# A grouped-scan convolution block on one core: one pair of units reordered where the pipeline fills, and two GpSimd outputs moved ahead of additions in the tail

## The chip, the cores and the metric

The kernel runs on one NeuronCore of one Trainium2 chip. The metric is device time in microseconds of one launch; the time before is the median of three runs. Engines are called PE (TensorE), DVE (VectorE), ACT (ScalarE), POOL (GpSimd) and SP (SyncE, which issues the DMAs here).

## The reference, cut to what matters

`x` is (4, 128, 96, 96) in float32. After a group norm, each of the four images is read as a sequence in four orders (rows, rows backward, columns, columns backward). On each sequence of 9216 positions a gated state-space block runs, and the four results are put back in place, joined by `fuse_w` and added to `x`:

```python
t = _grouped1x1(x, in_proj_w, in_proj_b, G)            # 128 -> 512, 4 groups
u, gate = t[:, :HID], t[:, HID:]
u = silu(u)
u = depthwise_conv(u, dw_w)                            # 5 taps along the sequence
s = _conv1x1(u, ssm_in_w)                              # 256 -> 32
a = DMIN + (DMAX - DMIN) * sigmoid(_conv1x1(u, ssm_delta_w, ssm_delta_b))
bb = tanh(_conv1x1(u, ssm_b_w, ssm_b_b))
cc = tanh(_conv1x1(u, ssm_c_w, ssm_c_b))
prefix = cumsum(log(a))
hst = exp(prefix) * cumsum(bb * s * exp(-prefix))      # h[n] = a[n] h[n-1] + bb[n] s[n]
u = u + _conv1x1(cc * hst + ssm_d[None, :, None] * s, ssm_out_w)
u = _grouped1x1(u * sigmoid(gate), mix_w, mix_b, G)
return _conv1x1(u, out_proj_w, out_proj_b)
...
x = x + fuse(concatenate(four results))
```

## The kernel before

**Units and pairs.** There are 8 phases: 4 images, each once as "V" and once as "H". A phase has 6 steps of 16 lines, and a step has 4 pairs. A pair is two units that run together, one forward (`s` = 0) and one backward (`s` = 1), each of N = 384 positions: every fourth position of a step, so that the phase of a position in the sequence is a separate array. In all there are 384 units and 192 pairs; `pair(t)` is called for t = 0 to 191, then `tail()`. The unit of pair t is i = 2t. Work on a unit is spread over pairs: `pair(t)` computes the front of pair t + 4, the convolution and projections of pair t, the scan results of pair t − 5, and the gates, state products and gating of pair t − LAG, with LAG = 6. The unit of that last one is called `bi`. So pair 6 is the first with `bi` = 0, the first in which gates and state products appear.

**Order.** All engines run in program order (`manual_schedule`), so the order of the calls is the order of each engine's queue, and an instruction that waits holds up all behind it. Waits are put in by the framework from the tiles and regions that instructions touch.

**What a pair does.** `front` makes four in_proj products per pair (L134, tiles of 32x32) into four PSUM banks, and ACT applies SiLU to each (L470). The depthwise convolution is done in two halves: channels of block 0 by PE with band matrices (`conv`, then `conv_less`), evicted by ACT to `u` (L616 or L618); channels of block 1 by DVE in taps (`taps`: the first tap by ACT at L635, four more by DVE at L637, in PSUM banks 0 and 1). `proj` makes s, a, bb and cc (L134 psum<-u,main), read by ACT at L674, L675 and L680; POOL multiplies them into the scan's inputs (L682, L683). DVE scans (L709), two halves per step. `outputs` forms cc * h and adds d * s: a multiplication (L715), an addition (L716) and a copy (L718), as a rule on POOL. `out_of` is the state product (L504, contraction of 32 rows), `gate` the product for the gate (L491, 32 rows), `sigmoids` the tanh of the gates (L521), `gating` the DVE work u = (gate + 1) * (u + state product) (L583 and L584). From pair 8 on `under` copies u into the PSUM bank ahead of the state product, and L583 is not needed. `accumulate` is the last product (L134 psum<-u,w_fin: mix, out_proj and fuse are one matrix), evicted by ACT as `ys` (L742, L744) and added to `acc` by POOL (L761), or added from PSUM by DVE (also L761) where `last` is set. `scale_s` is L692.

**PSUM.** There are 8 banks, given out by hand. Banks 0 to 3 hold the state products of the pair being gated (`SSM`), banks 0 and 1 also the taps. `FRONT` = (7, 6, 2, 3) are the banks of the front, `PROJ` = (4, 5) those of the convolution and projections, `GATE[True]` = (6, 4, 5, 7) those of the gates where a front runs in the same pair. So a bank passes several times in one pair from PE to ACT or DVE and back.

**Pair 6.** Here `bi` = 0 and a front is computed (step 2, group 2, called front 10 below; pair 7 computes front 11). The order of calls is `front(10, FRONT)`, taps and `conv`, `conv_less` with two copies, `outputs(2)`, `gates_and_out(0, True)`, `gating` of both units, `first_tap(14)`, `proj(12)`, `scale_s(10)`.

**Tail.** It finishes the pairs 186 to 191. `gate_units(n)` is the gating of pair n with `under` of pair n + 1; `product(n, 0, 4)` the last product of its forward unit into bank 4, added by POOL; `product(n, 1, 5)` that of the backward unit into bank 5, added by DVE when `add()` is called, which also issues the stores that are due; `z_copy` (L916) copies the scan result to the other half of the partitions for the state products. Two additions of pair 185 are held (`adds`). The outputs of pair 189 (`outputs(378, None, nc.vector)`) are on DVE, those of units 376, 380 and 382 on POOL:

```python
        ssm_out(first + 1)
        for held_add in adds:
            held_add()
        gate_units(first + 1)
        outputs(2 * first + 6, None, nc.vector)
        outputs(2 * first + 8, None)
        product(first, 0, 4)
        product(first, 1, 5)
        z_copy(first + 2)
        product(first + 1, 0, 4)
        outputs(2 * first + 10, None)
        add()
```

Here `first` = 186, so 2 * first + 6 is unit 378, + 8 unit 380 and + 10 unit 382.

Of the kernel before, what the change touches and what calls it, by code (L numbers as in the profile page):

```python
# [56 lines left out]
R = 4  # L57
LN = 16
NS = HH // LN
N = LN * WW // R  # L60
# [7 lines left out]
def conv_preact_kernel(  # L68
# [9 lines left out]
    nc = tc.nc  # L78
# [41 lines left out]
    psum = ps.tile([P, 8, 512], F32, name="psum")  # L120
    SSM, TAPS, PROJ = 0, 0, (4, 5)
# [379 lines left out]
    def out_of(bi, s, j):  # L501
        z = tbs[bi]
        r = slice(64 * j + 32 * s, 64 * j + 32 * s + 32)
        nc.tensor.matmul(bank(ssm(bi, s) + j)[:, :N], w_so[r, bass.ts(j, P)], z[r, :],  # L504
                         start=bi not in seeded, stop=True, skip_group_check=True)
# [8 lines left out]
    def sigmoids(bi, to):  # L514
        bn = stats[units[bi]["b"]][1]
        n = bi // 2
        gv = gates[n % 2]
        for s in range(2):

            for j in (0, 1) if s == 0 or to[0] == GATE[True][0] else (1, 0):  # L520
                nc.scalar.activation(  # L521
                    gv[:, s, j, :],
                    bank(to[2 * s + j])[:, :N],
                    AF.Tanh,
                    bias=bn[:, 2 + j : 3 + j],
                    scale=0.5,
                )
            load_gate(bi + s + UB)
        if n % NP < NP // 2 - 2:
            nc.sync.dma_start(kept[n // NP % 2][n % NP], gv)  # L530
# [19 lines left out]

    def gates_and_out(bi, with_front):

        to = GATE[with_front]
        gate(bi, 0, 0, to[0])
        gate(bi, 0, 1, to[1])
        if with_front:
            gate(bi, 1, 0, to[2])
            out_of(bi, 1, 0)
            out_of(bi, 0, 0)
            out_of(bi, 0, 1)  # L560
            out_of(bi, 1, 1)
            gate(bi, 1, 1, to[3])
        else:

            out_of(bi, 1, 0)
            gate(bi, 1, 0, to[2])
            out_of(bi, 1, 1)
            out_of(bi, 0, 1)
            out_of(bi, 0, 0)
            gate(bi, 1, 1, to[3])  # L570
        sigmoids(bi, to)

    def gating(bi, s):

        v = units[bi + s]["v"] = us[bi][:, s]
        m = mirror(bi // 2)
        if m is None:
            g = gates[bi // 2 % 2][:, s]
        else:
            g = old_gates.get(bi // 2, gates[m % 2])[:, 1 - s, :, ::-1]  # L580
        pz = psum[:, ssm(bi, s) : ssm(bi, s) + 2, :N]
        if bi not in seeded:
            nc.vector.tensor_add(pz, pz, v)  # L583
        nc.vector.scalar_tensor_tensor(v, g, 1.0, pz, ALU.add, ALU.mult)  # L584

# [20 lines left out]
    def conv_less(i, banks):  # L606
        step, p = units[i]["step"], units[i]["p"]
        sil, k, b0 = blocks(step), less_of(p), min(banks)
        for g in range(4):
            for s in range(2):  # L610
                r = less_rows(s, p)
                mm(bank(b0 + s), g, less[r, p, g, :], columns(step, sil[s][r, g, :], k),
                   False, True)
        if banks == PROJ:
            for s in range(2):
                nc.scalar.copy(us[i][:, s, 0, :], bank(b0 + s)[:, :N])  # L616
        else:
            nc.scalar.copy(us[i][:, :, 0, :], psum[:, b0 : b0 + 2, :N])  # L618
# [94 lines left out]
    def outputs(i, copy=nc.gpsimd.tensor_copy, engine=nc.gpsimd, r=slice(0, N)):  # L713
        ta, tb, p = scans[units[i]["step"]], tbs[i], units[i]["p"]
        engine.tensor_mul(ta[0:64, p, r], tb[64:P, r], ta[64:P, p, r])  # L715
        engine.tensor_add(tb[0:64, r], ta[0:64, p, r], tb[0:64, r])  # L716
        if copy:
            copy(tb[64:P, :], tb[0:64, :])  # L718
# [65 lines left out]
    def pair(t):  # L784
        i, k, bi = 2 * t, t % R, 2 * (t - LAG)
        back = bi >= 0
        old = back and mirror(bi // 2) is not None

        late = bi > 2 and (bi - 2) % (NU // B) == 0
        with_front = fresh((t + R) // R)  # L790
        final = (nc.vector, True) if t == NU // 2 - 1 else ()
        seed = old or back and not with_front

        ahead = old or back and not with_front
        banks, w = plan(with_front or not back)
        if not back:
            banks = head_banks(t)
        if back:
            front(t + R, FRONT)
        for n in soon:  # L800
            load_kept(n)
        soon.clear()
        if seed and not with_front:
            under(bi, 1)
        if t < NU // 2 - 2:
            send()

        if len(reload) == 4 and (k == 1 or late):
            for b, r in reload:
                nc.sync.dma_start(accf[:, r], xr[b, :, r])  # L810
            reload.clear()
        if t:
            new_u(i)
            taps(i, range(1, K))
            conv(i, banks)
        if t and not ahead:
            conv_less(i, banks)
        if not back and t:
            first_tap(i + 2)
            front(t + R, FRONT if banks == PROJ else (5, 4, 2, 3))  # L820
        recurrence(t)
        un = units[i]
        stats_chunks(t)

        ending = old and t % (2 * NP) > NP + NP // 2

        def stats_piece(at_end=False):
            if later and k > 1 and at_end == ending and t % (2 * NP) not in (27, 39):
                next(later[0], None)

        if not ahead:
            free[0] = w[1]
            stats_piece()
        if seed and with_front:
            for s in (1, 0):
                under(bi, s)
        for add in held:
            add()
        held.clear()
        if waiting:  # L840
            add = accumulate(waiting.pop(0), w[0], *final)
            if late:
                held.append(add)
            else:
                add()

        between = ahead and not old
        if between:
            conv_less(i, banks)
        if seed and not with_front:  # L850
            under(bi, 0)
        if ahead:
            accumulate(waiting.pop(0), w[1], *final)()
            free[0] = w[0]
            stats_piece()
            if not between:
                conv_less(i, banks)
        if old:
            scale_s(i - 2)
            for s in range(2):  # L860
                for j in range(2):
                    out_of(bi, s, j)
                load_gate(bi + s + UB)
        elif back:
            gates_and_out(bi, with_front)
        if back:
            for s in range(2):
                gating(bi, s)
        if un["order"] == "V" and un["b"] + 1 < B and un["st"] == NS - 1 and k == R - 1:
            later[:] = [stats_finish(un["b"] + 1)]  # L870
        if t + 2 < NU // 2:
            load_chunks(t + 2)
        if back:

            if k == 2 and t + 1 < NU // 2:
                soon.append(bi // 2 + 2)
            else:
                load_kept(bi // 2 + 2)
            if waiting:
                add = accumulate(waiting.pop(0), w[1])  # L880
                if late:
                    held.append(add)
                else:
                    add()
            first_tap(i + 2)
        if t == NU // 2 - 1:
            for s in range(2):
                under(bi + 2, s)
        if t == NU // 2 - 1:
            outputs(i - 8, None)  # L890
        if ending:
            free[0] = FRONT[0]
            stats_piece(True)
        proj(i, PROJ if back else banks, between)
        if not old and t > 0:
            scale_s(i - 2)
        if back:
            waiting.extend(units[bi : bi + 2])
        if t >= NU // 2 - 4:
            load_last(t)  # L900

        if bi > 0 and bi % (NU // B) == 0:
            send()

    def tail():
# [4 lines left out]
        def ssm_out(n):  # L910
            for s in range(2):
                for j in range(2):
                    out_of(2 * n, s, j)
# [24 lines left out]
        for part in range(2):  # L938
            scan(NU // UB - 1, part)
            outputs(2 * first + 4, None, r=bass.ts(part, N // 2))  # L940
        ssm_out(first + 1)
        for held_add in adds:
            held_add()
        gate_units(first + 1)
        outputs(2 * first + 6, None, nc.vector)
        outputs(2 * first + 8, None)
        product(first, 0, 4)
        product(first, 1, 5)
        z_copy(first + 2)
        product(first + 1, 0, 4)  # L950
        outputs(2 * first + 10, None)
        add()
        ssm_out(first + 2)
        for n in range(first + 2, end - 1):
# [226 lines left out]
```

## Time and profile before

| | |
|---|---|
| Median of 3 runs | 1815.12 us (1814.3 to 1817.42) |
| Profiled execution | 1815.66 us, its span 1813.9 us |
| Mean granted PE clock | 0.999 |
| Instructions | 56969, of them 24090 matmuls and as many weight loads |
| DMA | 321.17 MB, mean 177 GB/s |

The span runs from the first instruction to the last; the profiled execution's own time is longer by what lies around it. "Busy" is the time in which an engine executes, and PE's ends are modelled, so PE's busy time does not say that it runs at its peak. A timeline line gives start and length in us, engine, source line, operation, written and read tiles, shapes and count, and in brackets the idle time before it with what ended that. A line of waits gives who waited for whom, then total us, count and longest. A line of windows gives the stretch and its length, then busy us and instruction count of PE, PEld (weight loads), DVE, ACT and POOL, then the granted PE clock, the DMA share and GB/s.

### The profile page before, as it was taken

Reading aid. Unit: us, or ns where it says so; the run is one execution under the profiler, and the core shown is the slowest. Engines: PE = TensorE matmul, PEld = TensorE weight load, DVE = VectorE, ACT = ScalarE, POOL = GpSimd, SP = SyncE. Lnnn points to the kernel's source line nnn. Section 1 sums busy time; section 2 is a strip of 40 time slices with the busy share of each in tenths; the row PEclk is TensorE's granted clock in tenths of the full one; section 3 lists DMA queues with packets and bytes.
Section 4 is the critical chain, followed back from the end, with each engine's and each line's share of the span. In section 5 each row is a group of like instructions: output and inputs, shape, how many; then the busy total and the mean of one; then the engine's idle time right before and its main releaser. Section 6 shows DMA issues by size and latency. Waiting matters only on the chain.

```text
span 1813.9 us, 56969 instructions
## 1 busy us (share of the span) xinstructions
PE 1788.7 (99%) x24090; PEld 643.7 (35%) x24090; DVE 1448.5 (80%) x1462; ACT 1562.6 (86%) x2750; POOL 1431.1 (79%) x1477
## 2 busy tenths in 40 slices
PE   7999999999999999999999999999999999999998
PEld 3333333333333333333333333333333333333333
DVE  6888878787888887877778888787877788777886
ACT  4888888988888888898888888889888888888975
POOL 3587888788778888787877888878877788887786
PEclk9999999999999999999999999999999999999999
DMA  8555463444975466344696456443476634635434
GB/s 247 178 188 180 148 195 107 162 144 155 314 239 186 158 186 183 113 139 139 221 300 226 144 176 207 127 164 118 159 237 220 232 142 138 197 102 180 149 123 158
DMA packets 148047, 321.17 MB, mean 177 GB/s; under 512 B 14160, under 2 KB 115920, under 8 KB 147792
## 3 DMA queue, kind: packets, MB, share of 16 engines
q1 hardware_dynamic: 147648, 317.48, 54.1%
q8 instruction: 190, 3.11, 0.7%
q14 instruction: 65, 0.53, 0.1%
q10 hardware_dynamic: 144, 0.04, 0.0%
HBM read 185.21 MB, written 132.25 MB: 175 GB/s over the span
## 4 chain that ended last, share of the span: by engine, by line
PE 94%; DVE 2%; DMA 2%; ACT 1%; issue 0%; POOL 0%; SPq 0%; DVEq 0%; ACTq 0%; POOLq 0%
PE psum L134 81%; PE psum L504 8%; PE psum L491 5%; DVE psum L637 1%; DMA x_in<-in_xs 1%; DMA xs<-in_xr 1%; DVE u L584 0%; DMA acc<-in_xr 0%; DVE u L637 0%; ACT psum L635 0%; ACT psum L512 0%; ACT u L618 0%; ACT sil L470 0%; DVE t L715 0%; DVE t L709 0%
## 5 line engine op out<-in xcount | busy, mean ns | idle before, releaser
L637 DVE SCALAR_TENSOR_TENSOR psum<-sil,small,psum 128x768 f32<-128x768 f32 x576 | 589.0, 1022 | 28.3 <-ACT psum L635 3.4
L584 DVE SCALAR_TENSOR_TENSOR u<-gate,psum 128x768 f32<-128x768 f32 x376 | 349.6, 952 | 273.9 <-ACT u L616 122.4
L134 PE MATMUL psum<-u,w_fin 128*32 128x384 f32 (+1 forms) x6192 | 552.7, 486 | 3.5 <-DVE acc L761 2.1
L134 PE MATMUL psum<-u,main 128*32 128x384 f32 x6144 | 534.7, 489 | 1.2 <-DVE u L637 1.2
L761 POOL TENSOR_TENSOR acc<-ys,acc 128x384 f32<-128x384 f32 x375 | 411.7, 1119 | 27.9 <-ACT ys L744 8.4
L715 POOL TENSOR_TENSOR t<-t,t 64x384 f32<-64x384 f32 (+1 forms) x192 | 237.3, 1236 | 157.0 <-DVE t L709 73.3
L134 PEld LDWEIGHTS psum<-u,w_fin 128*32 128x32 f32 x6192 | 189.7, 110 | 322.6 <-issue 215.2
L134 PEld LDWEIGHTS psum<-u,main 128*32 128x32 f32 x6144 | 181.9, 109 | 324.5 <-issue 196.8
L512 ACT COPY psum<-u 128x768 f32<-128x768 f32 x352 | 276.8, 799 | 19.2 <-DVE u L637 11.3
L134 PE MATMUL psum<-sil,band 128*32 128x384 f32 x3072 | 285.1, 488 | 0.0
L682 POOL TENSOR_SCALAR t<-tm 64x384 f32<-64x384 f32 x191 | 177.0, 926 | 118.1 <-ACT tm L674 98.9
L716 POOL TENSOR_TENSOR t<-t,t 64x384 f32<-64x384 f32 (+1 forms) x192 | 248.8, 1296 | 15.1
L504 PE MATMUL psum<-t,main 32*128 32x384 f32 x1536 | 239.2, 513 | 1.3 <-ACT psum L512 0.6
L635 ACT ACTIVATE psum<-sil,small 128x768 f32<-128x768 f32 x191 | 173.2, 907 | 58.0 <-DVE u L584 49.7
L521 ACT ACTIVATE gate<-psum,bnorm 128x384 f32<-128x384 f32 x384 | 191.7, 581 | 27.0 <-PE psum L491 25.5
L683 POOL TENSOR_TENSOR t<-t,tm 64x384 f32<-64x384 f32 x192 | 195.1, 1016 | 15.3
L637 DVE SCALAR_TENSOR_TENSOR u<-sil,small,psum 128x768 f32<-128x768 f32 x192 | 194.9, 1015 | 7.8
L470 ACT ACTIVATE sil<-psum,bnorm 128x385 f32<-128x385 f32 x384 | 191.8, 584 | 3.9 <-PE psum L134 1.8
L134 PE MATMUL psum<-sil,less 64*32 64x384 f32 x3072 | 168.2, 495 | 0.0
L491 PE MATMUL psum<-x_in,wn 32*128 32x384 f32 x768 | 157.5, 527 | 0.4 <-ACT u L616 0.4
L134 PEld LDWEIGHTS psum<-sil,band 128*32 128x32 f32 x3072 | 90.6, 109 | 169.2 <-issue 95.0
L718 POOL COPY t<-t 64x384 f32<-64x384 f32 x187 | 136.5, 730 | 11.9
(102 smaller groups left out, 1477.2 us busy)
## 6 DMA issues: line engine op xcount, KB each, us to landing
sil<-sil SPq DMA_DIRECT2D x128, 770.0 KB, 6.9
kept<-gate SPq DMA_DIRECT2D x80, 768.0 KB, 3.7
gate<-kept SPq DMA_DIRECT2D x76, 768.0 KB, 4.8
x_in<-in_xs SPq DMA_DIRECT2D x192, 96.2 KB, 2.5
out<-acc SPq DMA_DIRECT2D x48, 384.0 KB, 8.5
acc<-in_xr SPq DMA_DIRECT2D x39, 384.0 KB, 6.4
xs<-in_xr SPq DMA_DIRECT2D x72, 192.0 KB, 5.8
x_in<-in_xs SPq DMA_DIRECT2D x46, 192.5 KB, 3.5
```

What stands on the lines that cost most here:

```text
L134: nc.tensor.matmul(o[r, : rhs.shape[-1]], lhsT, rhs, start=start, stop=stop, skip_group_check=True)
L470: nc.scalar.activation(sils[step][:, s, j, g, :], bank(bk)[:, : N + 1], AF.Silu, bias=bn[:, 1:2] if j else bn[:, 4 + g : 5 + g],)
L491: nc.tensor.matmul(bank(to)[:, :N], stats[un["b"]][0][r, s, :], x_in[s][r, q, off : off + N], start=True, stop=True)
L504: nc.tensor.matmul(bank(ssm(bi, s) + j)[:, :N], w_so[r, bass.ts(j, P)], z[r, :], start=bi not in seeded, stop=True, skip_group_check=True)
L512: nc.scalar.copy(psum[:, ssm(bi, s) : ssm(bi, s) + 2, :N], us[bi][:, s])
L521: nc.scalar.activation(gv[:, s, j, :], bank(to[2 * s + j])[:, :N], AF.Tanh, bias=bn[:, 2 + j : 3 + j], scale=0.5,)
L584: nc.vector.scalar_tensor_tensor(v, g, 1.0, pz, ALU.add, ALU.mult)
L637: nc.vector.scalar_tensor_tensor(us[i][:, :, 1, :] if k == K - 1 else part, src, w_tap[:, k : k + 1], part, ALU.mult, ALU.add,)
L683: nc.gpsimd.tensor_mul(ta[0:64, p, :], tb[0:64, :], tm[0:64, :])
L715: engine.tensor_mul(ta[0:64, p, r], tb[64:P, r], ta[64:P, p, r])
L716: engine.tensor_add(tb[0:64, r], ta[0:64, p, r], tb[0:64, r])
L761: adder.tensor_add(part, y, part)
```

## The change

In pair 6 (`bi` = 0) the front is computed in three pieces. Its in_proj goes into banks (2, 3, 7, 6) instead of (7, 6, 2, 3). The first two SiLUs, those of banks 2 and 3, stay ahead of the convolution; the other two come after `conv_less` and its copies. The four state products go ahead of the four gates, the gates use banks (4, 5, 7, 6), and DVE adds u to both units' state products before the first gating product. The change in `sigmoids` keeps the tanhs' order for this new set of banks at (0, 1). All other pairs are as before.

In the tail, `outputs` of unit 380 goes ahead of the two held additions, and `outputs` of unit 382 ahead of the products of pair 186 and 187, and so ahead of their additions on POOL. Nothing is added or taken out.

```diff
-            for j in (0, 1) if s == 0 or to[0] == GATE[True][0] else (1, 0):
+            for j in (1, 0) if s and to == GATE[False] else (0, 1):
...
     def gates_and_out(bi, with_front):
-        to = GATE[with_front]
+        to = GATE[with_front] if bi else (4, 5, 7, 6)
+        if bi == 0:
+            for s in range(2):
+                for j in range(2):
+                    out_of(bi, s, j)
+            for s in range(2):
+                for j in range(2):
+                    gate(bi, s, j, to[2 * s + j])
+            sigmoids(bi, to)
+            return
...
         pz = psum[:, ssm(bi, s) : ssm(bi, s) + 2, :N]
-        if bi not in seeded:
+        if bi == 0 and s == 0:
+            for e in range(2):
+                pe = psum[:, SSM + 2 * e : SSM + 2 * e + 2, :N]
+                nc.vector.tensor_add(pe, pe, us[bi][:, e])
+        elif bi and bi not in seeded:
             nc.vector.tensor_add(pz, pz, v)
...
-        if back:
+        if bi == 0:
+            turned = front_parts(t + R, (2, 3, 7, 6), half=True)
+            next(turned)
+            next(turned)
+        elif back:
             front(t + R, FRONT)
...
             conv_less(i, banks)
+        if bi == 0:
+            for _ in turned:
+                pass
...
         ssm_out(first + 1)
+        outputs(2 * first + 8, None)
         for held_add in adds:
             held_add()
         gate_units(first + 1)
         outputs(2 * first + 6, None, nc.vector)
-        outputs(2 * first + 8, None)
+        outputs(2 * first + 10, None)
         product(first, 0, 4)
         product(first, 1, 5)
         z_copy(first + 2)
         product(first + 1, 0, 4)
-        outputs(2 * first + 10, None)
         add()
```

## The prediction

> **What bounds the kernel now.** First the page: busy time, then the chain that ended last.
>
> ```profile
> PE 1788.7 (99%) x24090; PEld 643.7 (35%) x24090; DVE 1448.5 (80%) x1462; ACT 1562.6 (86%) x2750; POOL 1431.1 (79%) x1477
> ...
> PE 94%; DVE 2%; DMA 2%; ACT 1%; issue 0%; POOL 0%; SPq 0%; DVEq 0%; ACTq 0%; POOLq 0%
> ```
>
> The reader is to see that TensorE sets the time nearly everywhere: a change elsewhere pays only where PE stands still. So the next view is PE's waits, from 60 us to the end.
>
> ```profile
> PE psum L134 <- DVE acc L761: 2.1, 1, 2.1
> PE psum L134 <- ACT ys L742: 1.2, 1, 1.2
> PE psum L504 <- ACT psum L512: 0.6, 1, 0.6
> PE psum L134 <- DVE u L584: 0.6, 1, 0.6
> PE psum L491 <- ACT u L616: 0.4, 1, 0.4
> ```
>
> In 1750 us there are six waits, and three of them (2.1, 0.6, 0.4) lie where the change works: two in pair 6, one in the tail. PE's ends are modelled about 0.5 us late, so I count from start to start. PE's timeline in pair 6:
>
> ```profile
> 72.88 0.96 PE L491 MATMUL psum<-x_in,wn 32*128 32x384 f32 x2 [0.40 <-ACT u L616]
> ...
> 74.75 2.79 PE L134 MATMUL psum<-u,main 128*32 128x384 f32 x32
> 77.47 0.88 PE L134 MATMUL psum<-x_in,wn 32*32 32x385 f32 x16
> 78.92 0.88 PE L134 MATMUL psum<-x_in,wn 32*32 32x385 f32 x16 [0.57 <-DVE u L584]
> 79.73 0.53 PE L134 MATMUL psum<-sil,band 128*32 128x384 f32 x4
> ```
>
> The gates and state products start at 71.57 and projection at 74.75, 3.18 us later; in pair 7 the same stretch takes 1.58 (83.39 to 84.97). Then in_proj of front 11 is cut in two: banks 2 and 3 are held until VectorE's last product of the gating (L584) ends at 78.86. From conv (69.28) to conv (79.73) pair 6 takes 10.45 us. ScalarE in that stretch:
>
> ```profile
> 70.46 2.00 ACT L470 ACTIVATE sil<-psum,bnorm 128x385 f32<-128x385 f32 x4
> 72.33 0.88 ACT L616 COPY u<-psum 128x384 f32<-128x384 f32 x2
> 73.06 2.50 ACT L521 ACTIVATE gate<-psum,bnorm 128x384 f32<-128x384 f32 x4
> ```
>
> Four SiLUs stand ahead of the copies of u that free banks 4 and 5, and the gates wait for those banks. In the tail, VectorE and GpSimd:
>
> ```profile
> 1787.54 2.81 DVE L715 TENSOR_TENSOR t<-t,t 64x384 f32<-64x384 f32 x1
> 1787.65 1.95 POOL L761 TENSOR_TENSOR acc<-ys,acc 128x384 f32<-128x384 f32 x2
> ...
> 1789.67 1.73 POOL L715 TENSOR_TENSOR t<-t,t 64x384 f32<-64x384 f32 x1
> ...
> 1790.38 1.63 DVE L716 TENSOR_TENSOR t<-t,t 64x384 f32<-64x384 f32 x1
> ...
> 1791.94 0.54 DVE L761 TENSOR_TENSOR acc<-psum,acc 128x384 f32<-128x384 f32 x1
> ...
> 1792.53 0.87 PE L134 MATMUL psum<-u,w_fin 128*32 128x384 f32 x4 [2.14 <-DVE acc L761]
> ```
>
> VectorE's outputs of unit 378 (L715, L716) take 4.47 us, the addition that frees bank 5 is queued behind them, and PE waits for it. The clock by stretch adds a second price:
>
> ```profile
> 1788.88:1792.29 3.41, 1.51 (x18) 0.31 (x8) 3.38 (x3) 1.28 (x2) 3.25 (x3) 1.00 0.01 4
> 1792.29:1795.71 3.42, 3.18 (x20) 0.99 (x24) 2.23 (x4) 1.31 (x2) 3.34 (x4) 0.50 0.02 5
> ```
>
> After the wait PE runs at half clock (0.50) for 3.4 us. Its two products take 4.26 us there (1792.53 to the next L504 at 1796.79), the same work at full clock 2.72.
>
> **What the Trainium skill says.** "SBUF — State Buffer", Who interferes with whom: a VectorE instruction with two inputs in SBUF and a GpSimd one that reads SBUF exclude each other for the whole instruction. The trace agrees: VectorE's L715 ends 0.75 us after the second GpSimd addition, its L716 0.61 us after GpSimd's L715. "TensorE: Matmul & The Clock Gate", What's actually happening: the clock halves after an idle window of about 3.4 us on a free-running grid. The trace shows the same length (3.41 us at 0.50), but 2.1 us of idleness was enough here; 1.3 us (before 1788.04) was not. "TensorEngine Tiling (Array Packing)", Key Properties: matmuls on different row strips run side by side, and a change of tiling mode drains. Agrees: four state products on four strips take 0.86 us in the tail (1796.79 to 1797.65).
>
> **Pair 6, step by step.** Nothing is added or removed but the order and the banks.
> 1. ScalarE: SiLUs (0,0) and (0,1) at 70.46 to 71.52 as before. Conv_less starts at 70.71; in pair 7 the first copy of u follows its start by 0.97, so here at 71.68, not 72.33. The copies end at 72.16 and 72.54. SiLUs (1,0), (1,1) come after them, each 0.47 after the last: ends 73.01 and 73.48.
> 2. PE: the four state products need banks 0 to 3: last tap 71.35, SiLU (0,1) 71.52. They run at 71.57 to 72.33. The gates then wait for their banks one after another: 4 (72.2), 5 (72.6), 7 (73.05), 6 (73.52). From the last gate to projection it was 0.74 (74.01 to 74.75), so 73.52 + 0.74 = 74.3 against 74.75: only 0.45 saved, since the last SiLUs are now what is late.
> 3. VectorE: both additions run while ScalarE is at the gates: state products finish at 72.5, additions end 73.5 and 74.35. Tanhs end at 73.94, 74.41, 74.88, 75.35. So L584 ends at 75.4 and 76.35 instead of 76.93 and 78.86. Taps of pair 7, queued behind, end near 80.5, not 82.96.
> 4. In_proj of front 11 at 74.3 + 2.72 = 77.0: its banks 7, 6, 2, 3 are free at 76.35, so it runs whole, 0.97 as in pair 6. Conv at 77.98 against 79.73: **1.75 us saved**. Bank 5 for its second half: projection ends about 77.1, and the two ScalarE reads end at 78.2, before 78.6.
> The following SiLUs end at 80.8, so pair 7's copies of u end at 81.55, just before its gates at 81.6: nothing lost. Bounds: 0 if one of these banks is late, 2.6 if nothing waits (10.45 less 7.8 of PE work); I take 1.75. SP's queue keeps its order; the save of an older SiLU and the gate loads stay where they were, and their rows are needed four pairs on. From pair 8 on PE has no wait until the tail, so the gain is kept.
>
> **The tail.** Two mul and add pairs of GpSimd (2.4 us each) go ahead of the additions; no instruction is new.
> 1. VectorE's L715 is issued at 1787.54, while GpSimd's last half output runs to 1787.68. GpSimd's next was an addition, starting 0.03 before the end of the last, and so was the one after: VectorE got nothing until 1789.60. Now the next is a multiplication (L715), and ahead of each of those GpSimd leaves 0.08 us (1789.60 to 1789.67, 1786.15 to 1786.23): VectorE gets in, at about 1787.65.
> 2. VectorE's L715 ends near 1788.4 (0.61 to 0.75 after release), GpSimd's L715 near 1789.45 (1.06 later, as before), VectorE's L716 enters the gap there and ends near 1790.05 (0.61), not 1792.01. The addition ends at 1790.55 and PE starts at 1790.6 instead of 1792.53: **1.93 us**. PE itself is ready at 1790.33 (L504 at 1789.47 plus 0.86), so a faster VectorE would bring only 0.27 more. VectorE alone run without GpSimd is not in the trace; the bounds 0.5 and 0.95 give 1.7 to 2.1.
> 3. PE is then idle for 0.3 us, not 2.1, so the half clock should go: 4.26 − 2.72 = **1.54 us**. Bounds 0 and 1.7 (half of 3.41).
> 4. What is delayed: the held additions end near 1793.0 (were 1789.6), the next two at 1797.4 (were 1794.9). Their readers: the buffers of ys are wanted again at about 1793.5 and 1797, and four stores on SP start at 1797.4, taking some 4.5 us, before the last stores at about 1804. Both covered. Additions on VectorE touch other rows or columns of acc. Afterwards each unit takes 3.58 us as now.
>
> **Sum.** The profiled execution took 1815.66 (span 1813.9 and 1.8 around it). 1815.66 − 1.75 − 1.93 − 1.54 = 1810.44. It lies 0.5 above the median 1815.12, inside the runs shown (1814.3 to 1817.42); whether the half clock falls in every run isn't known, and a median run without it gains less from a lower start. I take **1810.4**.
>
> **Rivals.**
> B, only pair 6 pays: the tail's wait moves from the addition to another resource, or the reorder does nothing for VectorE. Against: the gap before each L715. 1815.66 − 1.75 = 1813.9.
> C, only the tail pays: a SiLU after the copies makes the last gate late, up to 0.9 us on PE. For: step 2 leaves ScalarE the limit. 1815.66 − 3.47 = 1812.2.
> D, slower: VectorE loses the gap. If its L715 comes after GpSimd's at 1787.76 (0.22 later than now), it ends at 1789.6, its L716 stands behind GpSimd's L716, both held additions (no gap between) and, if that gap is lost too, the multiplication of 382: 1794.35. PE at 1794.9 is 2.4 late, with the half clock up to 0.15 dearer; if pair 6 then brings nothing, 1818.2, with its gain 1816.5. Against: both engines are timed from the end of the same scan (1785.65).
>
> **Chances.** A 0.72 (1809.3 to 1811.8), B 0.10, C 0.09, D 0.09. 0.2% is 3.6 us, about what a measurement of this kernel can tell from no change: faster lies below 1811.5, which holds nearly nine tenths of A and a little of C, 0.64; slower, above 1818.75, a D that loses more than reckoned, 0.04; the rest 0.32. The range 1808.9 to 1813.3 leaves out D, most of B and a thin lower end of A, 0.2 in all.
>
> **What would show it.** Right: conv to conv in pair 6 near 8.7 us, no wait for L584; VectorE's L715 and L716 together 2.5 us, PE's wait for L761 under 0.4, no 0.50 clock before 1800. Wrong: projection of pair 6 after 74.75, a VectorE L716 over 2 us, or a new wait for ys or bank 6.

## The result, and the profile after

The changed kernel takes 1811.53 us (median of 13 runs, 1809.72 to 1817.25), the kernel before 1815.39 in as many runs (1814.03 to 1817.58): ratio 0.9978, 95% interval 0.9971 to 0.9986. That is 3.9 us less, by the interval 2.5 to 5.3; the forecast was 1810.4, 5.2 below the execution it was reckoned from. The profiled execution took 1814.41 us, with a span of 1812.7.

The page after, busy time:

```profile
PE 1788.9 (99%) x24090; PEld 645.3 (36%) x24090; DVE 1446.5 (80%) x1462; ACT 1567.0 (86%) x2750; POOL 1432.0 (79%) x1477
```

Counts of instructions and busy times are nearly those of before, as they should be for a change of order. What has changed is where PE stands still. PE's waits from 60 us to the end (who waited for whom, total us, times, longest):

```profile
PE psum L134 <- ACT ys L755: 1.2, 1, 1.2
PE psum L504 <- ACT psum L512: 0.6, 1, 0.6
PE psum L134 <- DVE acc L774: 0.3, 1, 0.3
PE psum L134 <- ACT t L693: 0.2, 1, 0.2
```

Lines have moved down: L742 is L755 now, L761 is L774, L583 and L584 are L596 and L597, L616 is L629, L715 and L716 are L728 and L729. Of the three waits that the prediction aimed at, the 2.1 us of the tail are 0.3 and those of pair 6 (0.6 and 0.4) are gone. PE's timeline in pair 6, and below it one line each of ScalarE's and VectorE's:

```profile
72.99 1.50 PE L134 MATMUL psum<-sil,band 128*32 128x384 f32 x16
...
75.23 0.96 PE L504 MATMUL psum<-t,main 32*128 32x384 f32 x8
75.98 2.18 PE L491 MATMUL psum<-x_in,wn 32*128 32x384 f32 x8
78.09 2.79 PE L134 MATMUL psum<-u,main 128*32 128x384 f32 x32
80.81 0.94 PE L134 MATMUL psum<-x_in,wn 32*32 32x385 f32 x32
81.69 1.50 PE L134 MATMUL psum<-sil,band 128*32 128x384 f32 x16
```

```profile
75.39 0.86 ACT L629 COPY u<-psum 128x384 f32<-128x384 f32 x2 [0.16 <-PE psum L134]
...
78.18 1.90 DVE L597 SCALAR_TENSOR_TENSOR u<-gate,psum 128x768 f32<-128x768 f32 x2
```

The state products run first and wait for nothing, in_proj stands in one block of 32, and from conv (72.99) to conv (81.69) it is 8.70 us where it was 10.45. VectorE's last gating product (L597) is done at 80.08, before in_proj asks for its bank. Pair 7 then takes 9.20 us (next conv at 90.89), 0.07 more than before. Both pairs together gain 19.58 − 17.90 = 1.68 us.

In the tail, VectorE, then GpSimd, then PE (start, length, engine, line, operation, tiles):

```profile
1789.79 0.89 DVE L728 TENSOR_TENSOR t<-t,t 64x384 f32<-64x384 f32 x1
1790.71 1.68 DVE L729 TENSOR_TENSOR t<-t,t 64x384 f32<-64x384 f32 x1
1792.32 0.53 DVE L774 TENSOR_TENSOR acc<-psum,acc 128x384 f32<-128x384 f32 x1
...
1790.02 1.74 POOL L728 TENSOR_TENSOR t<-t,t 64x384 f32<-64x384 f32 x1
...
1792.90 2.79 PE L134 MATMUL psum<-u,w_fin 128*32 128x384 f32 x32 [0.26 <-DVE acc L774]
```

VectorE's multiplication takes 0.89 us instead of 2.81: it gets in ahead of GpSimd's multiplication, where before it stood behind two GpSimd additions (e4 below tests this). Since all kernels differ a little at their start, tail times below are counted from the end of the last scan. PE's product, which waited for the addition, starts at 5.00 (before: 6.88), a gain of 1.88. It runs at full clock: 2.72 us to the next L504, where the profiled execution of before had 4.26. The tail ends 24.79 after the scan, before 28.22.

One thing in this profile was not in the forecast, whose sign "no 0.50 clock before 1800" holds in the tail alone. The windows around 26 us (stretch, length, busy us of PE, PEld, DVE, ACT, POOL, then the granted clock):

```profile
22.47:25.88 3.41, 2.97 (x90) 1.54 (x97) 0.85 (x5) 2.35 (x6) 0.00 (x0) 1.00 0.64 160
25.88:32.71 6.83, 6.83 (x70) 4.63 (x55) 0.99 (x6) 4.79 (x10) 0.81 (x1) 0.50 0.28 76
```

This execution spends 6.83 us at half clock while the pipeline fills, long before the changed code, and the conv of pair 5 starts at 66.14 instead of 62.45. Half clock for 6.83 us can cost up to 3.4 of these 3.69 us, an estimate from the window above. So its span is only 1.2 us shorter although pair 6 and the tail together gain 1.68 + 3.43. Counted from the conv of pair 5 to the end of the span, the kernel takes 1746.56 us, before 1751.42: 4.86 less.

### The profile page after: what moved, and what is told of

Its sections match the earlier page's. It is cut to its first block, busy times and chain, and to the rows that moved or that the text cites. A ratio compares the mean times of both kernels' runs of the same rounds, so it can differ in the third digit from the quotient of the medians.

```text
span 1812.7 us, 56970 instructions
## 1 busy us (share of the span) xinstructions
PE 1788.9 (99%) x24090; PEld 645.3 (36%) x24090; DVE 1446.5 (80%) x1462; ACT 1567.0 (86%) x2750; POOL 1432.0 (79%) x1477
## 4 chain that ended last, share of the span: by engine, by line
PE 95%; DMA 2%; DVE 2%; ACT 1%; issue 0%; SPq 0%; DVEq 0%
PE psum L134 82%; PE psum L504 8%; PE psum L491 5%; DVE psum L650 1%; DMA x_in<-in_xs 1%; DMA xs<-in_xr 1%; DMA acc<-in_xr 0%; DVE u L597 0%; DVE u L650 0%; ACT psum L512 0%; PE psum L1035 0%; ACT u L631 0%; SPq L296 0%; ACT ys L757 0%; DVE bn L387 0%
## 5 line engine op out<-in xcount | busy, mean ns | idle before, releaser
L597 DVE SCALAR_TENSOR_TENSOR u<-gate,psum 128x768 f32<-128x768 f32 x376 | 350.0, 953 | 273.4 <-ACT u L629 119.0
L774 POOL TENSOR_TENSOR acc<-ys,acc 128x384 f32<-128x384 f32 x375 | 411.6, 1119 | 24.0 <-ACT ys L757 7.9
L728 POOL TENSOR_TENSOR t<-t,t 64x384 f32<-64x384 f32 (+1 forms) x192 | 237.7, 1238 | 156.9 <-DVE t L722 73.2
L729 POOL TENSOR_TENSOR t<-t,t 64x384 f32<-64x384 f32 (+1 forms) x192 | 249.1, 1297 | 15.0
L504 PE MATMUL psum<-t,main 32*128 32x384 f32 x1536 | 238.6, 513 | 1.3 <-ACT psum L512 0.6
```

The costliest lines, as they stand in the source:

```text
L774: adder.tensor_add(part, y, part)
```

## The experiments

**Each part alone.** e1 keeps pair 6 as changed and the tail of before; e2 keeps pair 6 of before and the changed tail. e1, against the changed kernel:

```diff
         ssm_out(first + 1)
-        outputs(2 * first + 8, None)
...
-        outputs(2 * first + 10, None)
+        outputs(2 * first + 8, None)
...
         product(first + 1, 0, 4)
+        outputs(2 * first + 10, None)
```

> Only pair 6 is changed, the tail is that of before. Theory (two separate parts, each worth its own PE stall): conv to conv of pair 6 is 8.70 us as in the changed kernel, PE waits about 2.1 us for the DVE addition in the tail, and the time is 1.75 us below before (ratio 0.9990). Rival B': the gain of pair 6 is given back later by a transfer or by the tail, then the ratio is 1.000 though the stretch of pair 6 is short. Its trace is also one more look at whether PE falls to half clock after the 2.1 us wait.

> Only the tail is changed, pair 6 is that of before. Theory: pair 6 takes 10.45 us, PE's wait for the DVE addition is 0.3 us, no half clock there; the time is 1.9 us below before in executions of before without the half clock and 3.4 us in those with it, so between 0.9981 and 0.9990 as a ratio. Rival: the tail pays only together with pair 6 (a shifted phase of engines), then the wait of 2.1 us is back.

e1: 1812.6 us median, ratio 0.999 (0.9982 to 0.9998). Conv to conv is 8.70 and pair 7 9.19, and of this gain nothing is lost on the way: from the conv of pair 5 to that of pair 191, e1 takes 1.68 us less than the profiled execution of before. The tail is that of before (VectorE's multiplication 2.76 us, PE at 6.83, half clock after it). e2: 1811.72, ratio 0.9986 (0.9978 to 0.9994). Pair 6 takes 10.46; PE's product starts at 5.00 and the tail ends at 24.79, both exactly as in the changed kernel. The kernel before had 1814.3 beside both. So both parts pay and neither depends on the other: rivals B and C, with one part each, fall.

**Is it the half clock?** e3 leaves the kernel before as it is and fills PE's wait in the tail with two matmuls on weights whose sums nobody reads:

```diff
         ssm_out(first + 2)
+        for _ in range(2):
+            nc.tensor.matmul(bank(4), w_main[:, 0:P], w_main[:, 0:512], start=True, stop=True)
```

> The kernel before, with two matmuls of 128x512 on weights added into bank 4 after the state products of pair 188, in the time in which PE stood still for 2.1 us; their result is overwritten by the next product. Theory (the half clock comes of the idle time): PE still waits for the DVE addition and starts at the same distance from the scan, but runs at full clock, 2.72 us from that start to the next state products and not 4.26; the time is 0 to 1.5 us below before, by how often before falls to half clock. Rival (the half clock comes of something else, such as the stores or DVE and POOL at work): still 0.50 for 3.4 us, and the time 0 to 0.3 us above before.

The window that holds the wait, and PE's product after it, both of e3:

```profile
1795.35:1798.76 3.41, 3.20 (x24) 1.12 (x28) 3.41 (x4) 0.93 (x2) 3.33 (x3) 1.00 0.02 5
```

```profile
1797.42 2.79 PE L134 MATMUL psum<-u,w_fin 128*32 128x384 f32 x32 [0.21 <-DVE acc L761]
```

The product starts at 6.87 as in the kernel before, yet runs at full clock, and the tail ends at 26.67, 1.55 us sooner. Without the two matmuls PE would have stood still for 2.07 us of that one window (1795.35 to 1797.42), about as long as in b2 below, whose clock fell. So the half clock there comes of PE's idleness. But the timed gain is nothing that can be seen: 1813.53, ratio 0.9999 (0.999 to 1.0007). A saving of 1.5 us in every run would be 0.9992; the interval just holds that too, so the times alone don't settle it. They raise the question whether every run of the kernel before has a half clock there to lose.

**How often?** b2 and b3 are the kernel before, profiled twice more.

> The kernel before, unchanged, for one more look at its tail. The prediction implies that PE's 2.1 us of waiting is followed by a stretch of 3.4 us at half clock in every execution: then the second-last ssm_out comes about 11.1 us after the end of the last scan. Rival (only some executions have it, by where the wait falls against the clock's windows): about 9.6 us, full clock.

> The kernel before once more, for the same question: 11.1 us from the end of the last scan to the second-last ssm_out if the half clock always follows the wait, 9.6 us if not.

The windows with the wait and after it, first of b2, then of b3:

```profile
1792.65:1796.06 3.41, 1.30 (x16) 0.41 (x18) 3.38 (x4) 1.23 (x2) 3.31 (x3) 1.00 0.00 0
1796.06:1799.47 3.41, 3.41 (x24) 1.06 (x20) 1.67 (x3) 1.31 (x2) 3.25 (x4) 0.50 0.23 86
```

```profile
1789.49:1792.90 3.41, 2.14 (x24) 0.57 (x16) 3.38 (x2) 1.55 (x3) 3.25 (x4) 1.00 0.05 18
1792.90:1796.32 3.42, 2.55 (x32) 0.94 (x32) 3.01 (x5) 1.31 (x2) 3.34 (x4) 1.00 0.02 5
```

The wait is the same in both (2.11 and 2.14 us). In b2 it lies whole in one window, from 1793.39 to 1795.50, leaves PE 1.30 us busy of 3.41, and the next window runs at 0.50. In b3 a border of the grid, counted in steps of 3.413 from the drop at its end (1813.38), cuts it at 1792.90 into 1.27 and 0.87; neither half is enough, and the second-last ssm_out comes at 9.60, not at about 11.2. The Trainium skill, "TensorE: Matmul & The Clock Gate", What's actually happening, says that the window is free-running; this agrees, and shows that where a fixed wait falls on the grid decides.

The mean granted clock that each run reports gives the share: of 57 runs of the kernel before that stood beside these experiments, 30 have 1.000 (median 1813.5), 18 have 0.999 (median 1815.4, 1.8 more), 9 have less. One window at half clock, 1.7 us of 1814, leaves 0.9991, so the 30 had none. But 0.999 doesn't say where the window lies: kernels without that wait have it too, in 8 of 62 runs (e2 1 of 21, the changed kernel 1 of 13, e3 3 of 13, e9 2 of 6, e10 1 of 9), and in e7's profile it comes of the last 2.55 us alone, after PE's work. So the tail's half clock fell in fewer than half of the runs (at most 27 of 57); a third, the 18, is an estimate, and a fifth would be left of it if 0.999 came from elsewhere as often as in those kernels. The profiles are too few to say: of the four with that wait (before, e1, b2, b3) three have it.

**Who lets VectorE in?** e4 puts one held addition ahead of the moved output, the other after it:

```diff
         ssm_out(first + 1)
+        adds[0]()
         outputs(2 * first + 8, None)
-        for held_add in adds:
-            held_add()
+        adds[1]()
```

> The changed kernel with the first of the two held additions put back ahead of the output of unit 380 on GpSimd. GpSimd's work up to the later one is the same. Theory (VectorE and GpSimd exclude each other and VectorE gets in only where GpSimd pauses): the multiplication on VectorE is held through the first addition, ends 0.9 to 1.0 us later relative to the end of the scan, and PE's wait for the VectorE addition grows from 0.26 to 1.2 us. Rival (both share bandwidth, or what counts is that the outputs are early at all): the wait stays at 0.3 to 0.5 us.

VectorE's multiplication in e4, and GpSimd's addition and multiplication beside it:

```profile
1785.23 1.86 DVE L728 TENSOR_TENSOR t<-t,t 64x384 f32<-64x384 f32 x1
...
1785.33 1.00 POOL L774 TENSOR_TENSOR acc<-ys,acc 128x384 f32<-128x384 f32 x1
1786.40 1.74 POOL L728 TENSOR_TENSOR t<-t,t 64x384 f32<-64x384 f32 x1
```

It lasts one GpSimd addition longer (1.86 against 0.89), and PE starts at 5.93, 0.93 later than in the changed kernel. With no addition ahead, one, and two, the multiplication takes 0.89, 1.86 and 2.81: VectorE waits for whole GpSimd additions to `acc`, one after another, and gets in ahead of the first multiplication, where GpSimd pauses for 0.07 us (1786.33 to 1786.40). It is not the kind of operation alone: in the changed kernel VectorE's own addition gets in ahead of GpSimd's output addition, where GpSimd pauses as well (1791.76 to 1791.84). That the pause is what lets it in fits each of these cases, but no run changes the pause alone. PE's wait of 1.19 us brought no half clock. Its one run took 1810.79 us.

**Which step of pair 6 pays?** Each of the next three undoes one thing in the changed kernel: e5 puts the gates ahead of the state products again, e6 computes all four SiLUs ahead of the convolution, e7 puts the additions of u back to each unit's gating.

```diff
e5:              for j in range(2):
-                    out_of(bi, s, j)
+                    gate(bi, s, j, to[2 * s + j])
...
-                    gate(bi, s, j, to[2 * s + j])
+                    out_of(bi, s, j)
e6:          turned = front_parts(t + R, (2, 3, 7, 6), half=True)
-            next(turned)
-            next(turned)
+            for _ in turned:
+                pass
e7:      pz = psum[:, ssm(bi, s) : ssm(bi, s) + 2, :N]
-        if bi == 0 and s == 0:
...
-        elif bi and bi not in seeded:
+        if bi not in seeded:
```

> The changed kernel with the four gates of pair 6 ahead of its four state products; banks and the split of the front as changed. Theory (state products first are what lets VectorE start early): the additions start after the last gate, about 2.8 us later, the last gating product ends near 6.1 us after conv_less begins plus 2.3, in_proj of front 11 is held again for banks 7 or 2 and 3, and conv to conv is 10.3 to 10.7 us. Rival (the split front and the early copies of u are what counts): 8.7 to 9.4 us.

> The changed kernel with all four SiLUs of front 10 ahead of the convolution, as before; banks and the order of state products and gates as changed. My sum gives: copies of u 0.65 us later, gates of banks 4 and 5 with them, those of banks 7 and 6 no longer late, projection held by the tanh that frees bank 4, conv to conv 8.8 us: the split is worth only 0.1 us. Rival (the split is what makes the gates early, as the waits of the trace of before suggest): 9.2 to 9.4 us.

> The changed kernel with VectorE's two additions in the old order (addition, gating product, addition, gating product). Theory (VectorE has 0.7 us to spare when in_proj of front 11 comes): the second gating product ends 1.0 us later, in_proj is split and conv to conv is 8.9 to 9.0 us. Rival (VectorE is the bound of pair 6): 9.6 to 9.7 us. If the additions do not matter: 8.70.

Conv to conv, from one profile of each:

| | pair 6 | pair 7 | both | lost against the changed kernel |
|---|---|---|---|---|
| before | 10.45 | 9.13 | 19.58 | 1.68 |
| changed | 8.70 | 9.20 | 17.90 | |
| e5, gates first | 9.83 | 9.60 | 19.43 | 1.53 |
| e6, front whole | 8.76 | 9.18 | 17.94 | 0.04 |
| e7, additions as before | 8.94 | 9.13 | 18.07 | 0.17 |

The order of gates and state products carries nearly all. In e5 PE waits for the copy of u:

```profile
76.70 1.92 PE L491 MATMUL psum<-x_in,wn 32*128 32x384 f32 x7 [0.62 <-ACT u L629]
```

The state products come behind that wait, so VectorE's gating ends later, and the loss is paid in two pairs: 1.13 here, 0.40 in pair 7. Of the 1.13, 0.64 lie ahead of projection, which starts 5.74 after conv (changed: 5.10), and 0.49 in in_proj, which takes 1.37 us to the next conv instead of 0.88 while VectorE's last gating product runs until 8.97 after conv (changed: 7.09). In pair 7 conv is 0.16 longer and the stretch of gates and state products 0.25. The mechanism is the expected one; the 9.83 us of pair 6 lie below the 10.3 to 10.7 that were expected. In e6 the gates wait for that copy too, but after the state products, and it costs almost nothing:

```profile
75.97 1.30 PE L491 MATMUL psum<-x_in,wn 32*128 32x384 f32 x8 [0.40 <-ACT u L629]
77.54 2.79 PE L134 MATMUL psum<-u,main 128*32 128x384 f32 x32 [0.28 <-ACT gate L521]
```

Projection starts 5.16 after conv, in the changed kernel 5.10: it waits for ScalarE's tanhs, and ScalarE has the same work in either order. Each of these runs takes one step out of the whole change, so it shows what the change loses without that step and not what the step brings alone. The new banks of the front and of the gates were not undone by themselves. The single times (1816.81, 1813.53, 1809.1) can't be set beside each other: e5 had 10.24 us at half clock in the start, e6 6.83, e7 none.

**Which of the two outputs?** e8 leaves unit 382 where it was and moves only unit 380.

```diff
-        outputs(2 * first + 10, None)
...
         product(first + 1, 0, 4)
+        outputs(2 * first + 10, None)
         add()
```

> The changed kernel, but only the output of unit 380 goes ahead of the held additions; that of unit 382 stays behind the products of pairs 186 and 187. Theory (the gain comes of the multiplication that stands next to VectorE's): PE's wait for the VectorE addition 0.26 us as in the changed kernel, and the same distance from there to the end. Rival (both outputs have to be early, for state products of pair 190 and 191 wait for them): a new PE wait at the last state products, 0.5 us or more.

PE starts at 4.98, the tail ends at 24.77: the same as with both. The second move does nothing for the time.

**A further step.** PE is ready at 4.7, so freeing VectorE further can only pay if PE's earlier wait, 1.2 us for `ys`, goes too. e9 puts the addition of unit 373 (pair 186's backward unit) on VectorE between the multiplication and the addition of unit 378, and the product of unit 372 with ScalarE's copy of its sums between ScalarE's two `under` copies. The expectation calls these units 375 and 374.

```diff
-        gate_units(first + 1)
-        outputs(2 * first + 6, None, nc.vector)
+        gating(2 * n, 0)
+        under(2 * n + 2, 0)
+        add_first = accumulate(units[2 * first], 4)
+        gating(2 * n, 1)
+        under(2 * n + 2, 1)
+        wait.append(accumulate(units[2 * first + 1], 5, nc.vector, True))
...
+        nc.vector.tensor_mul(ta[0:64, p, :], tb[64:P, :], ta[64:P, p, :])
+        wait.pop(0)()
+        nc.vector.tensor_add(tb[0:64, :], ta[0:64, p, :], tb[0:64, :])
...
-        product(first, 0, 4)
-        product(first, 1, 5)
+        add_first()
...
-        add()
```

> The changed kernel, and in the tail VectorE's addition of unit 375, which frees bank 5, stands between the multiplication and the addition of unit 378's outputs, with the ScalarE copies of unit 374's sums put between the two copies of state-product sums ahead of it; the order of the other additions is unchanged. Theory (VectorE's queue set the time, and after the change what PE waits for is ScalarE's and VectorE's order, not GpSimd): the second product of PE starts about 3.5 us after the end of the last scan where the changed kernel has 5.0, the second-last ssm_out about 6.9 instead of 7.7, and the stretch from the scan's end to the span's end takes about 23.9 us instead of 24.8; about 0.9 us less than the changed kernel, ratio to the kernel before near 0.9974. Rival (VectorE gets its turn beside GpSimd only in the two pauses, and a third instruction that doesn't fall into them waits): the multiplication or the addition goes back to 2 us or more, and the tail is 1 to 2.4 us longer than the changed kernel's.

VectorE in e9:

```profile
1785.87 0.93 DVE L974 TENSOR_TENSOR t<-t,t 64x384 f32<-64x384 f32 x1
1786.83 0.56 DVE L774 TENSOR_TENSOR acc<-psum,acc 128x384 f32<-128x384 f32 x1
1787.30 1.23 DVE L976 TENSOR_TENSOR t<-t,t 64x384 f32<-64x384 f32 x1
```

The addition from PSUM takes 0.56 us (0.53 in the changed kernel) while GpSimd's multiplication is under way (2.10 to 3.89), and VectorE's own addition still catches GpSimd's pause and ends at 4.55. PE's second product starts at 3.47, the second-last ssm_out at 6.98, and the tail ends at 24.05, 0.74 sooner than in the changed kernel where 0.9 was expected. Timed: 1810.05 median of 6 runs, before 1815.07, ratio 0.9975 (0.996 to 0.9991). The trace shows the gain; the intervals of this kernel and of the changed one overlap, so the timing alone does not. The two moves were not tried apart.

**The half clock in the start.** e10 is e9 with two more idle matmuls while the pipeline fills. The expectation places both in the first 15 us; in the trace the second runs at 24.14 us, between the first in_proj products.

```diff
-        for n in (512, 512):
+        for n in (512, 512, 512):
...
-        for g in range(R):
+        in_proj(0, 0, 0, 0, banks[0][0][0])
+        filler(512)
+        in_proj(0, 0, 1, 0, banks[0][0][1])
+        for g in range(1, R):
             burst(0, g)
```

> The kernel of the run before, and in the first 15 us PE gets two more idle matmuls of 128x512 (a third one ahead of the second group of start-up pieces, one between the first two in_proj products); nothing else is touched. Theory (the stretch of half clock near 25 us that some looks show comes of idle time of PE in the start, as the one in the tail does): such a stretch becomes rarer, the times lie closer together, and the median is 0 to 1.5 us below the run before's. Rival (it doesn't depend on PE's idle time there): the spread stays as it is, and the two matmuls delay the start by 0.3 to 0.5 us.

Median 1811.21, above e9's, but 9 runs within 1809.79 to 1811.87; ratio 0.9973 (0.9963 to 0.9983). None of the nine has a mean clock under 0.999; of the changed kernel's 13 runs three have, and of e9's 6 one. With so few runs, nine without one could be chance. That the filler removes the half clock of the start is not shown. In the one profile the conv of pair 5 starts at 64.52, 2.09 later than in e9; other profiles without a half clock in the start have it anywhere from 60.97 to 64.08, so what the two matmuls cost isn't known either.

## Why the prediction was right, and where it was off

**Pair 6: right, to a tenth.** Two readings were off without effect on the sums: the groups of PE shown end 0.07 us behind the next start where nothing waits (74.75 + 2.79 = 77.54 against 77.47), not 0.5, and PE's idle time ahead of 1788.04 is 1.2 us by the waits shown there, not 1.3. The forecast counts from conv at 69.28 and the trace after from conv at 72.99. Copies of u done: 3.26 forecast, 3.26 measured. Tanhs done: 6.07 and 6.10. L597 done: 7.07 and 7.09. Projection: 5.02 and 5.10. Next conv: 8.70 and 8.70. That the last pair agrees to the hundredth is luck: projection came 0.08 late, and from there to the next conv it took 3.60 us instead of 3.68. Step 1, that the split SiLUs make the copies early, came true but adds almost nothing to the gain (e6: 0.04); what step 2 said, that ScalarE's late work then decides, holds even more than was thought. The gain comes of steps 2 and 3, state products ahead of gates (e5) and the additions under ScalarE's work (e7).

**Pair 7: a small miss.** "Nothing lost" was 0.07: the copies of u came out just ahead of the gates in the working, and in the trace the pair takes 9.20 instead of 9.13. In e7, with the additions as before, it takes 9.13. Net 1.68 instead of 1.75.

**Tail, steps 1 and 2: right.** From the scan's end, forecast and measured: VectorE's multiplication ends at 2.75 and 2.77, its addition at 4.40 and 4.48, PE starts at 4.95 and 5.00. The gain is 1.88 instead of 1.93, and e4 shows the mechanism. Rival D, that VectorE loses its turn, did not happen: both engines are timed from the end of one scan, as was argued.

**Tail, step 3: the term that was mis-sized.** 1.54 us for the half clock were taken in full, since the profiled execution had it. In an execution that has it, it is worth that (e3: 1.55). But the sum is a forecast of a median, and b3 and the mean clocks show that more than half of the runs of the kernel before don't have it: at a third of the runs it is worth about 0.5 on the mean, an estimate (0.3 at a fifth, 0.7 at 27 of 57). The prediction named the doubt and still counted it whole. With the other terms as measured, 1.68 + 1.88 + 0.5 = 4.1 us against 3.9 measured. Among the runs with a mean clock of 1.000 the two parts alone show without it: e1 1811.6 and e2 1811.3, the kernel before on that chip 1813.3, thus 1.75 and 2.0 us, with 1.68 and 1.88 in the traces. The profiles say the same: from the conv of pair 5 to the end of the span the changed kernel takes 4.86 us less than the profiled execution of before, which had the half clock in the tail, and 3.26 less than b3 (1749.82), which had not. The measured 3.86 lies between.

**Tail, step 4: right.** The held additions end at 7.44 (forecast 7.35), and PE has no wait for them.

**Left over.** The forecast fall was 5.22 us, the measured one 3.86. Of the 1.36 between them the half clock makes 1.0 and pair 7 and the tail 0.1; the rest is less than the measurement can tell, since the interval alone is 2.5 to 5.3 and the start makes single runs differ by up to 5 us (the conv of pair 5 starts at 67.38 in e3, with 10.24 us at half clock, and at 62.45 in the profiled execution of before). Not all scatter is the clock's: b2 lost 1.38 us between the convs of pairs 50 and 51 at full clock, and the profile names no cause. The forecast gave 0.64 to a fall of more than 0.2%; measured are 0.22%, by the interval 0.14 to 0.29, so on which side it lies can't be told.

## What to carry to other kernels

Before a stall seen in one profile is priced, ask whether it is in every run: two more profiles of the same kernel would have shown it in one and not in the other (b2, b3), and the clock of each timed run would have turned 1.5 us into about 0.5. Where VectorE and GpSimd exclude each other, look at what GpSimd does next, not only at how long VectorE takes: each addition queued there made VectorE's 64x384 multiplication about 0.96 us longer, and PE's wait with it. And where an engine's queue holds products for two others, put first the one whose inputs are ready and whose reader is late: without the state products ahead of the gates the change loses 1.53 us, without the split front 0.04 and without the early additions 0.17.

## What the runs showed of the hardware

- The clock of PE fell after windows of 3.41 us in which PE was busy for 1.30 (b2), 1.32 (e1) and 1.51 us (before), and not after ones with 1.79 (e4, 1802.51 to 1805.92) and 2.14 (b3); between 1.51 and 1.79 nothing was measured. The Trainium skill, "TensorE: Matmul & The Clock Gate", What's actually happening, speaks of an idle window; here a window that was busy for over a third of its length was enough, and the measurement decides.
- In the start the clock fell also after a window in which PE counted as busy for 2.97 of 3.41 us (four other runs: e3 2.84, e5 2.85, e6 2.95 and e2 3.14), and stayed down for two or three windows. One with 2.65 (after, 19.05 to 22.46) did not bring it down. So the share of busy time is not all that decides; what else does is open.
- GpSimd kept VectorE out through additions to `acc` that follow one another without a pause (they overlap by about 0.04 us in the trace), for 0.95 to 0.97 us each. It let VectorE in where it paused for 0.07 to 0.08 us: ahead of its output multiplication and of the output addition behind it.
- A VectorE addition with one input in PSUM was not held up by GpSimd (0.56 us in e9 beside a GpSimd multiplication). That agrees with the Trainium skill, "SBUF — State Buffer", Who interferes with whom, by which a VectorE instruction with at most one SBUF input does not contend with GpSimd.
